# Two-layer graph attention on one core: layer 0's values in one visit, row logits ahead of the output projection, and a new order of the start

## The chip, the cores and the metric

The kernel runs on one core of a Trainium2 chip. The metric is the device time of one execution in microseconds (us); lower is better. All tensors are float32 unless said otherwise.

## The reference

There are 64 graphs of N = 256 nodes with F = 512 features and an adjacency matrix each. Two layers follow each other, each with a residual sum and a layer norm.

```python
# layer 0: graph attention with 8 heads of 64 units
feats   = einsum('bnf,hfu->bhnu', x, W)
e_self  = einsum('bhnu,hu->bhn', feats, a_self)
e_neigh = einsum('bhnu,hu->bhn', feats, a_neigh)
dense   = leaky_relu(e_self[..., :, None] + e_neigh[..., None, :], 0.2) - 1e10 * (1 - adj)
out     = relu(softmax(dense) @ feats + b)             # heads side by side: 512 wide
x       = layernorm(x + out)
# layer 1: 8 heads of 64; attention plus adjacency plus a function of it
q, k, v = x @ W_qkv                                    # 512 -> 3 x 512
attn    = 0.33 * softmax(q k^T / 8, masked) + 0.33 * adj + 0.33 * exp(-adj)
x       = layernorm(x + (attn @ v) @ W_out + b_out)
```

## The kernel before, in words

**Three graphs are in work at once.** The main loop runs b from 1 to 63. In one turn it does layer 0's attention of graph b beside layer 1's projections of graph b-1 (`attention0_beside_projections1`), then layer 1's scores of graph b-1 and the values and output of graph b-2 beside layer 0's projections of graph b+1 (`attention1_beside_projections0`). `start()` does graph 0 and the first products, `end()` the last ones. The order on every engine is written out by hand: the helper `do(stage, graph, step, ...)` issues a step and then `in_order()` ties each new instruction to the one before it on its engine. Each engine works its own list in that order, and so does SP, which issues nearly all transfers. An instruction that waits holds up everything behind it on its engine.

**The large products are made in seven parts** (`seven`, a Strassen-like scheme): p1 to p7 are products of halves and of sums of halves. They write three PSUM banks: `chain` gathers p1, p6, p7 and p4 in turn and ScalarE copies it out after each (L309); `alone` holds p2; `pair` holds p5 and then also p3. VectorE adds a bank to what ScalarE has copied (L312): `add 11` takes p2, `add 22` takes the pair after p5, `add 12` takes it after p3. So p3 must wait for `add 22`, and p6, p7 and p4 for the copy before them. This is done three times per graph: `pq` (q and k of layer 1), `pv` (its values), `pf` (features of layer 0). The adds are called qk_add, v_add and add.

**Layer 0's attention of graph b**, by the names in the profile:
- `pr` (L82): four transposes bring the two row logits of each head into rows. They read `v` (the tile V0 with features and logits), to which VectorE has added the bias (`bias`, L569). VectorE takes a maximum (L489, L490), ScalarE an exponential (L491), VectorE clamps it (L494).
- `gs`, `gb`: SP stores these 8 rows to DRAM (8 KB) and reads them back broadcast to 128 partitions (1,028 KB). `gb` has one buffer.
- `nd` (L543): the column logits less the maximum that came with `gb`; ScalarE makes `ccol` and a factor of the values from it (L550, L551), and scales the values of each head by the factor (`scaled`, L610, 16 instructions).
- `pT` (`weights`, L646): VectorE makes the unnormalised weights of a head as max(gb, ccol) times the mask, two instructions a head.
- `av` (`product`, L669): TensorE multiplies weights and values. A product writes 64 of the 128 columns of the array. Heads 0 to 3 are group 0, heads 4 to 7 group 1; each group has its own PSUM tile, and the profile shows 64 matmuls a group.
- `norm0` (L682, L684), `end` (L695): division by the sum, then relu, residual and the sums for the norm; POOL makes the mean (L346), ScalarE the squares and the norm (L351, L367). The result `x` goes to DRAM and comes back in blocks (`hs`, `hb`), and VectorE turns these to `hT` (L121) and makes the sums of halves `hC`.

**Layer 1's attention:** `pz` are the scores of a pair of heads, `p` their exponentials (ScalarE, L822), `both` the sums over two tiles (VectorE, L834), `pd` the denominators (TensorE, L842). From `zd` on (L863 to L875) VectorE inverts them; `rs` and `rb` carry them through DRAM and back, broadcast (1,024 KB). `weights` of attend1 (L901, L908) multiplies by `rb` and adds `ct`, the function of the adjacency matrix (`shared`, L456 to L471, from `adjT`). `av` at L918 are the values, `po` the output projection (L1003), summed into `x` by L931. `store` normalises graph b-3 (two L367) and sends it out.

**One turn on TensorE before:** pq p1, p2, p6, p5, p7; av group 0; pq p4, p3; av group 1; pv and pf mixed; pz 0, 1; av (L918); pz 2, 3; po; pr; po; pd.

**On VectorE before**, from pd on: zd to rec, four sums xC, nd, eight pT (heads 0 to 3), qk_add 11, qk_add 22, eight pT (heads 4 to 7), norm0 of group 0, attend1's weights 0, qk_add 12, norm0 of group 1, end, v_add 11, weights 1, v_add 22, weights 2 and so on.

**PSUM** has four banks that all small products share in turn (`ps_tile`, tag `mm`) and two tiles of two banks for `av`, `pz` and the start's broadcast `pg` (tag `sc`).

**In the start**, graph 0's and graph 1's row factors are broadcast on TensorE (`pg`, L532). Its features (L579) are done without the seven parts, and the four steps of `attention_vectors` put the products of weights and attention vectors in extra columns of the weights (`pw`, `pwa`, with `a2` from `acol`, L399). `right_factors` makes the four sums of weights for `pf` (L218 to L221, tile wf) and for `pv`.

Of the kernel before, what the change touches and what calls it, by code (L numbers as in the profile page):

```python
# [17 lines left out]
def kernel(  # L18
# [29 lines left out]
    nc = tc.nc  # L48
# [331 lines left out]
    def attention_vectors(g, step):  # L380
# [14 lines left out]
        if step == 1:  # L395
            if g == 0:
                for r in range(2):
                    rows = slice(r * U, (r + 1) * U)
                    nc.vector.tensor_copy(  # L399
                        a2[rows, :, r, :].rearrange("p g s -> p s g"), acol[rows]  # L400
                    )
# [3 lines left out]
        if step == 2:  # L405
            pwa = WA[g, "logits"]
# [22 lines left out]
    def proj0(b):  # L429
# [52 lines left out]
        def rows():  # L482
            pr = ps_tile([H, 2, N], f"pr_{b}")
            for s in range(2):
# [5 lines left out]
            nc.vector.tensor_scalar_mul(nb, grow[:, N : N + 1], -0.8)  # L490
            nc.scalar.activation(  # L491
                grow[:, :N], pr[:, 0, :], AF.Exp, bias=nb, scale=-0.8
# [115 lines left out]
        def scaled(h):  # L608
# [18 lines left out]
            rows=rows,  # L627
            columns=columns,
# [9 lines left out]
    def attend0(b):  # L638
        pT = {}

        def weights(h):

            tag = "pT" if b > 1 or h < HG else "p" if h < HG + 2 else "both"
            pT[h] = work.tile([P, T, N], FT, tag=tag, name=f"pT_{b}_{h}", bufs=4)
# [402 lines left out]
    def start():  # L1047
# [3 lines left out]
        for g in range(2):  # L1051
# [4 lines left out]
            if g == 0:  # L1056
                do("proj0", 0, "aT")
                load_adj(1)
                do("proj0", 0, "far")
# [4 lines left out]
        do("turned", 1, "xT")  # L1064
        do("proj0", 0, "columns")
        do("proj0", 0, "factors")
        attention_vectors(1, 1)
        attention_vectors(0, 2)
        attention_vectors(1, 2)
        attention_vectors(2, 0)  # L1070
        attention_vectors(3, 0)
        for h in range(2):
            do("proj0", 0, "scaled", h)
            do("attend0", 0, "weights", h)
# [4 lines left out]
        for h in range(2, HG):  # L1079
            do("proj0", 0, "scaled", h)  # L1080
            do("attend0", 0, "weights", h)
        do("proj0", 1, "features", 0, 0)
        do("proj0", 1, "features", 0, 1)
        do("attend0", 0, "product", 0, 0)
        do("attend0", 0, "product", 0, 1)
        for h in range(HG, H):
            do("proj0", 0, "scaled", h)
            do("attend0", 0, "weights", h)
        do("proj0", 1, "features", 1, 0)
        do("attend0", 0, "product", 1, 0)  # L1090
        do("attend0", 0, "product", 1, 1)
# [11 lines left out]
        for t in range(T):  # L1103
            for g in range(2):
                do("proj0", 1, "copied", t, g)
# [256 lines left out]
```

## Time and profile before

| | us |
|---|---|
| time, median of 3 runs | 2990.06 (2988.39 to 2990.53) |
| profiled execution, its own time | 2991.16 |
| its span, first to last instruction | 2989.4 |
| TensorE busy (PE) | 2957.4 |
| VectorE busy (DVE) | 2610.0 |
| ScalarE busy (ACT) | 1478.2 |
| one turn of the loop, undisturbed | 45.36 |
| first turn's pq starts at | 113.90 |
| mean granted clock of TensorE | 0.993 of full |

In the profile PE is TensorE's matmuls and PEld its weight loads, DVE is VectorE, ACT is ScalarE, SPq the queue that issues transfers. A timeline row has the start, the time from the first instruction's start to the last one's end, engine, line, operation, out<-in and the count; in brackets stands the idle time before it and what ended it. A matmul's record runs on while the next one has begun, so the length of a piece of work on TensorE is read from one row's start to the next row's start. A row of waits has the engine, the waiting line, what it waited for, the total in us, how often, and the longest. A row of windows has the stretch, its length, the busy time and count of PE, PEld, DVE, ACT and POOL, the granted clock, the DMA share and GB/s.

### The profile page before, as it was taken

How to read it: one execution, taken by the hardware profiler on the slowest of the kernel's cores; microseconds unless marked ns; L12 is line 12 of the kernel's file. 1: busy time of each engine (PE TensorE's matmuls, PEld its weight loads, DVE VectorE, ACT ScalarE, POOL GpSimd, SP SyncE). 2: the span in 40 equal slices, each digit the busy share in tenths (PEclk: the TensorE clock that was granted, in tenths of full speed). 3: DMA queues.
4: the chain of work that ended last, by engine and by line, in shares of the span. 5: the costliest groups of instructions: out<-in, count | busy, mean ns of one | idle time of the engine just before them, and what ended most of it. 6: DMA issues, size and time to landing. Idle time of an engine off the chain costs nothing.

```text
span 2989.4 us, 64730 instructions
## 1 busy us (share of the span) xinstructions
PE 2957.4 (99%) x25526; PEld 2332.6 (78%) x25526; DVE 2610.0 (87%) x5151; ACT 1478.2 (49%) x3585; POOL 183.5 (6%) x526
## 2 busy tenths in 40 slices
PE   8899999999999999999999999999999999999998
PEld 7777877877878778778778778788787787787775
DVE  5889888889888888888888888888988988888885
ACT  2454554455455455455545544554554555455443
POOL 0000000000000000000000000000000000000000
PEclk7999999999999999999999999999999999999999
DMA  6353454444444444444534544444444435445431
GB/s 120 86 128 99 109 130 98 111 126 104 111 122 103 116 109 107 125 102 110 129 96 109 133 97 111 122 104 115 110 108 123 108 105 129 97 108 133 96 93 50
DMA packets 760613, 328.22 MB, mean 110 GB/s; under 512 B 693516, under 2 KB 694268, under 8 KB 744312
## 3 DMA queue, kind: packets, MB, share of 16 engines
q1 hardware_dynamic: 758200, 323.55, 43.5%
q8 instruction: 204, 3.34, 0.5%
q14 instruction: 97, 0.79, 0.1%
q10 hardware_dynamic: 2112, 0.52, 0.1%
HBM read 256.13 MB, written 67.61 MB: 108 GB/s over the span
## 4 chain that ended last, share of the span: by engine, by line
PE 92%; DVE 3%; DMA 3%; ACT 1%; issue 1%; SPq 0%; POOL 0%; DVEq 0%; POOLq 0%
PE pq_p L300 25%; PE po L1003 14%; PE pf_p L300 13%; PE pv_p L300 12%; PE pz L813 8%; PE av L669 8%; PE av L918 7%; PE pd L842 2%; DMA gb<-gs 1%; PE pr L82 1%; DMA out_dram<-x 1%; DVE p L908 0%; DVE p L901 0%; PE pg L532 0%; DMA gs<-grow 0%
## 5 line engine op out<-in xcount | busy, mean ns | idle before, releaser
L300 PE MATMUL pq_p<-hC,wqk_sb 128*128 128x128 f32 x4096 | 487.1, 277 | 2.0 <-ACT qk L309 1.9
L300 PEld LDWEIGHTS pq_p<-hC,wqk_sb 128*128 128x128 f32 x4096 | 468.9, 192 | 7.7 <-ACT qk L309 2.9
L1003 PE MATMUL po<-wo_sb,oT 128*128 128x512 f32 x1024 | 466.3, 599 | 0.0
L646 DVE SCALAR_TENSOR_TENSOR pT<-gb,ccol,at 128x256 f32<-128x256 f32 x992 | 403.2, 480 | 17.6 <-ACT ccol L550 17.6
L300 PEld LDWEIGHTS pq_p<-hT,wqk_sb 128*128 128x128 f32 x3072 | 355.9, 193 | 29.6 <-DVE hC L278 23.9
L300 PE MATMUL pq_p<-hT,wqk_sb 128*128 128x128 f32 x3072 | 373.6, 278 | 3.2 <-DVE hT L121 1.9
L822 ACT ACTIVATE p<-pz,hide 128x512 f32<-128x512 f32 x512 | 310.8, 691 | 123.9 <-PE av L918 106.7
L1003 PEld LDWEIGHTS po<-wo_sb,oT 128*128 128x128 f32 x1024 | 184.7, 190 | 207.5 <-issue 205.8
L309 ACT COPY v<-pv_p 128x256 f32<-128x256 f32 x256 | 95.5, 373 | 472.6 <-PE pv_p L300 472.5
L351 ACT ACTIVATE junk<-x,nmean_l 128x512 bf16<-128x512 f32 x256 | 185.6, 725 | 279.9 <-POOL nmean_l L346 275.8
L908 DVE TENSOR_TENSOR p<-p,ct 128x1024 f32<-128x1024 f32 x252 | 308.7, 1225 | 8.6
L901 DVE TENSOR_TENSOR p<-p,rb 128x1024 f32<-128x1024 f32 x252 | 304.5, 1208 | 5.2 <-DMA rb<-rs 5.2
L669 PE MATMUL av<-v,pT 128*64 128x65 f32 x8192 | 267.1, 223 | 0.6 <-DVE pT L646 0.6
L669 PEld LDWEIGHTS av<-v,pT 128*64 128x64 f32 x8192 | 249.3, 138 | 16.5 <-issue 1.4
L610 ACT ACTIVATE v<-v 128x64 f32<-128x64 f32 x1024 | 260.3, 342 | 0.0
L813 PE MATMUL pz<-qk 64*128 64x256 f32 x2048 | 256.2, 389 | 0.6 <-ACT p L822 0.5
L300 PE MATMUL pf_p<-wf_sb,xC 128*128 128x264 f32 x992 | 252.3, 387 | 0.0
L300 PE MATMUL pv_p<-wv_sb,hC 128*128 128x256 f32 x1024 | 244.4, 381 | 5.5 <-DVE v L312 5.3
L813 PEld LDWEIGHTS pz<-qk 64*128 64x128 f32 x2048 | 187.1, 186 | 65.1 <-ACT p L822 25.6
L918 PE MATMUL av<-p,v 128*64 128x256 f32 x2016 | 231.7, 382 | 0.0
L300 PEld LDWEIGHTS pv_p<-wv_sb,hC 128*128 128x128 f32 x1024 | 193.4, 190 | 37.8 <-DVE v L312 10.7
L309 ACT COPY qk<-pq_p 128x512 f32<-128x512 f32 x256 | 147.7, 577 | 141.5 <-PE pq_p L300 141.4
(137 smaller groups left out, 3806.2 us busy)
## 6 DMA issues: line engine op xcount, KB each, us to landing
rb<-rs SPq DMA_DIRECT2D x63, 1024.0 KB, 4.6
gb<-gs SPq DMA_DIRECT2D x62, 1028.0 KB
xb<-in_x_dram SPq DMA_DIRECT2D x252, 128.0 KB, 4.1
x<-in_x_dram SPq DMA_DIRECT2D x63, 512.0 KB
hs<-x SPq DMA_DIRECT2D x63, 512.0 KB
hb<-hs SPq DMA_DIRECT2D x252, 128.0 KB, 3.4
out_dram<-x SPq DMA_DIRECT2D x63, 512.0 KB, 4.4
adj<-in_adj_dram SPq DMA_DIRECT2D x256, 64.0 KB, 4.5
```

The source lines that it names most:

```text
L300: matmul(d, lhsT, rhs, start=(p in FIRST and i == 0), stop=(i == len(todo) - 1), skip_group_check=True,)
L309: nc.scalar.copy(out[COPIES[p]], dst)
L351: nc.scalar.activation(junk, self.src[:, t, :], AF.Square, bias=self.nmean[:, t : t + 1], accum_out=self.rstd[:, t : t + 1],)
L610: nc.scalar.activation(V0[b][:, t, h, :U], V0[b][:, t, h, :U], AF.Copy, scale=V0[b][:, t, h, U : U + 1],)
L646: nc.vector.scalar_tensor_tensor(pT[h][:, j, :], GB[b][h], CCOL[b][:, j, h : h + 1], AT[b][:, j, :], op0=ALU.max, op1=ALU.mult,)
L669: matmul(av[r * half : (r + 1) * half, k, :], pT[h][:, j, i : i + half], V0[b][:, j, h, :UA], start=(j == 0), stop=(j == T - 1),)
L813: matmul(pz[:, r, j, :], QK[b][rows, g, 1, j * P : (j + 1) * P], QK[b][rows, g, 0, :], start=True, stop=True,)
L822: nc.scalar.activation(p[:, :, j, :], pz[:, :, j, :], AF.Exp, bias=hide[:, j, b : b + 1], scale=U**-0.5,)
L901: nc.vector.tensor_mul(p, p, REC[b][:, k : k + 2, g // 2, :] .unsqueeze(2) .to_broadcast([P, 2, T, N]),)
L908: nc.vector.tensor_add(p, p, CT[b].unsqueeze(1).to_broadcast([P, 2, T, N]))
L918: matmul(av[0][r * U : (r + 1) * U, g % 2, :], V1[b][:, j, 2 * g + r, :], PROBS[b][g][:, r, j, :], start=(j == 0), stop=(j == T - 1),)
L1003: matmul(po, oT[:, c, t * P : (t + 1) * P], wo_sb[:, c, :], start=(c == 0), stop=(c == C - 1),)
```

## The change

In the loop's first half, `av` of both groups of graph b is issued together, between p7 and p4 of `pq`. For that the weights of heads 4 to 7 are made right behind qk_add 11 and ahead of qk_add 22, and they get buffers of their own (tag `both`) in place of those of heads 0 to 3. The `store` of graph b-3 is issued ahead of p6; attend1's weights 0 come ahead of norm0, norm0 and `end` directly one behind the other, then load(b+2), then p4 and p3; attend1's weights 1 come ahead of the values.

In the second half, `rows` (pr and the maximum) is issued behind the scores 3 and ahead of `both` 2 and 3; its second part, now a step of its own called `broadcast` (exponential, clamp, gs, gb), follows them; both stand ahead of the residual sum and `po`.

In the start, all eight heads' weights of graph 0 are made directly after their row factors, and `av` of graph 0 is done there, with the columns' products (`attention_vectors`) between and behind its two groups; graph 1's features come after it. load(2), `ct` of graph 0, adjT of graph 1, `xT` of graph 2 and the sums of wf are issued earlier, ahead of `copied` of graph 1. `xT` and `xC` of graph 2 and the sums of wf no longer stand in the first turn and at the start's end (xC stays at the start's end).

```diff
             wT = WA[g] = work.tile([P, C, P], FT, tag="both", name=f"wT_{g}", bufs=4)
             nc.scalar.copy(wT, pw)
         if step == 1:
-            if g == 0:
-                for r in range(2):
-                    rows = slice(r * U, (r + 1) * U)
-                    nc.vector.tensor_copy(
-                        a2[rows, :, r, :].rearrange("p g s -> p s g"), acol[rows]
-                    )
             pwa = WA[g, "logits"] = ps_tile([P, C, 4], f"pwa_{g}")
             for c in range(C):
                 matmul(pwa[:, c, :], WA[g][:, c, :], a2[:, g], start=True, stop=True)
         if step == 2:
             pwa = WA[g, "logits"]
             for k in range(2):
                 nc.vector.tensor_copy(
...
             nb = small.tile([H, 1], FT, tag="nb", name=f"nb_{b}", bufs=2)
             nc.vector.tensor_reduce(grow[:, N : N + 1], pr[:, 1, :], AX.X, ALU.max)
             nc.vector.tensor_scalar_mul(nb, grow[:, N : N + 1], -0.8)
+            ROW.update(logits=pr, rows=grow, shift=nb)
+        def broadcast():
+            grow = ROW["rows"]
             nc.scalar.activation(
-                grow[:, :N], pr[:, 0, :], AF.Exp, bias=nb, scale=-0.8
+                grow[:, :N], ROW["logits"][:, 0, :], AF.Exp, bias=ROW["shift"], scale=-0.8
             )
             nc.vector.tensor_scalar(
                 grow[:, :N], grow[:, :N], 1.0, TINY, op0=ALU.min, op1=ALU.max
...
 
         def weights(h):
 
-            tag = "pT" if b > 1 or h < HG else "p" if h < HG + 2 else "both"
-            pT[h] = work.tile([P, T, N], FT, tag=tag, name=f"pT_{b}_{h}", bufs=4)
+            tag = "pT" if h < HG else "both" if b > 1 or h > HG + 1 else "p"
+            if (b, h) == (0, H - 1):
+                pT[h] = work.tile([P, T, N], FT, tag="rec1", name=f"pT_{b}_{h}", bufs=1)
+            else:
+                pT[h] = work.tile([P, T, N], FT, tag=tag, name=f"pT_{b}_{h}", bufs=4)
             for j in range(T):
                 nc.vector.scalar_tensor_tensor(
                     pT[h][:, j, :],
...
                 do("proj0", 0, "logits", t, g)
                 do("proj0", 0, "copied", t, g)
             if g == 0:
+                for r in range(2):
+                    rows = slice(r * U, (r + 1) * U)
+                    nc.vector.tensor_copy(
+                        a2[rows, :, r, :].rearrange("p g s -> p s g"), acol[rows]
+                    )
                 do("proj0", 0, "aT")
                 load_adj(1)
                 do("proj0", 0, "far")
...
         do("proj0", 0, "maxima")
         attention_vectors(0, 1)
         do("turned", 1, "xT")
+        load(2)
         do("proj0", 0, "columns")
         do("proj0", 0, "factors")
+        for h in range(H):
+            do("proj0", 0, "scaled", h)
+            do("attend0", 0, "weights", h)
+        for t in range(T):
+            do("attend0", 0, "product", 0, t)
         attention_vectors(1, 1)
+        attention_vectors(2, 0)
+        for t in range(T):
+            do("attend0", 0, "product", 1, t)
+        attention_vectors(3, 0)
         attention_vectors(0, 2)
         attention_vectors(1, 2)
-        attention_vectors(2, 0)
-        attention_vectors(3, 0)
-        for h in range(2):
-            do("proj0", 0, "scaled", h)
-            do("attend0", 0, "weights", h)
+        for t in range(T):
+            for g in range(2):
+                do("attend0", 0, "norm0", g, t)
+            do("attend0", 0, "end", tiles[t])
+            do("attend0", 0, "squares", tiles[t])
         attention_vectors(2, 1)
         attention_vectors(3, 1)
         attention_vectors(2, 2)
         attention_vectors(3, 2)
-        for h in range(2, HG):
-            do("proj0", 0, "scaled", h)
-            do("attend0", 0, "weights", h)
-        do("proj0", 1, "features", 0, 0)
-        do("proj0", 1, "features", 0, 1)
-        do("attend0", 0, "product", 0, 0)
-        do("attend0", 0, "product", 0, 1)
-        for h in range(HG, H):
-            do("proj0", 0, "scaled", h)
-            do("attend0", 0, "weights", h)
-        do("proj0", 1, "features", 1, 0)
-        do("attend0", 0, "product", 1, 0)
-        do("attend0", 0, "product", 1, 1)
-        do("proj0", 1, "features", 1, 1)
-        do("attend0", 0, "norm0", 0, 0)
-        do("attend0", 0, "norm0", 0, 1)
         combine_weights1(0)
-        do("attend0", 0, "norm0", 1, 0)
-        do("attend0", 0, "end", tiles[0])
-        do("attend0", 0, "squares", tiles[0])
-        do("attend0", 0, "norm0", 1, 1)
-        do("attend0", 0, "end", tiles[1])
-        do("attend0", 0, "squares", tiles[1])
+        for t in range(T):
+            for g in range(2):
+                do("proj0", 1, "features", t, g)
         do("attend0", 0, "norm", tiles[0])
+        do("proj0", 0, "shared")
+        do("proj0", 1, "aT")
+        load_rows(1)
+        do("turned", 2, "xT")
+        right_factors(wf_sb, wf12)
+        in_order()
         for t in range(T):
             for g in range(2):
                 do("proj0", 1, "copied", t, g)
-        load_rows(1)
         do("proj0", 1, "maxima")
         do("proj0", 1, "columns")
-        do("proj0", 0, "shared")
-        do("proj0", 1, "aT")
         do("proj1", 0, "from_rows", 0)
         do("attend0", 0, "norm", tiles[1])
         do("proj1", 0, "qk", "p1")
...
         do("proj0", 1, "factors")
         combine_weights1(1)
         combine_weights1(2)
-        load(2)
         load_adj(2)
         do("proj1", 0, "qk_add", 11)
         do("proj1", 0, "qk", "p6")
...
         do("proj1", 0, "qk", "p4")
         do("proj1", 0, "qk", "p3")
         do("proj1", 0, "qk_add", 12)
-        right_factors(wf_sb, wf12)
-        in_order()
+        do("turned", 2, "xC")
 
     def attention0_beside_projections1(b):
 
...
             do("proj1", b - 1, "qk", "p1")
             do("proj1", b - 1, "qk", "p2")
             do("proj0", b, "columns")
+            do("attend1", b - 3, "store")
             do("proj1", b - 1, "qk", "p6")
             for h in range(HG):
                 do("proj0", b, "scaled", h)
                 do("attend0", b, "weights", h)
-            do("attend1", b - 3, "store")
             do("proj1", b - 1, "qk_add", 11)
+            for h in range(HG, H):
+                do("proj0", b, "scaled", h)
             do("proj1", b - 1, "qk", "p5")
+            for h in range(HG, H):
+                do("attend0", b, "weights", h)
             do("proj1", b - 1, "qk", "p7")
             do("proj1", b - 1, "qk_add", 22)
-        do("attend0", b, "product", 0, 0)
-        do("attend0", b, "product", 0, 1)
-        if b > 1:
-            for h in range(HG, H):
-                do("proj0", b, "scaled", h)
-            do("proj1", b - 1, "qk", "p4")
-            for h in range(HG, H):
-                do("attend0", b, "weights", h)
-        do("attend0", b, "norm0", 0, 0)
-        do("attend0", b, "norm0", 0, 1)
-        do("attend1", b - 2, "weights", 0)
-        if b > 1:
-            do("proj1", b - 1, "qk", "p3")
-            do("proj1", b - 1, "qk_add", 12)
-        else:
-            do("turned", b + 1, "xT")
-            do("turned", b + 1, "xC")
+            do("attend1", b - 2, "weights", 0)
+        for g in range(2):
+            for t in range(T):
+                do("attend0", b, "product", g, t)
+        if b == 1:
             do("proj0", b, "shared")
             load_rowmask()
             nc.sync.dma_start(bo_bc, b_out.partition_broadcast(P))
             nc.sync.dma_start(wo_sb, w_out.rearrange("(c p) f -> p c f", p=P))
             in_order()
+        for g in range(2):
+            for t in range(T):
+                do("attend0", b, "norm0", g, t)
+        do("attend0", b, "end")
         if b + 2 < NB:
             load(b + 2)
-        do("attend0", b, "product", 1, 0)
-        do("attend0", b, "product", 1, 1)
+        if b > 1:
+            do("proj1", b - 1, "qk", "p4")
+            do("proj1", b - 1, "qk", "p3")
+            do("proj1", b - 1, "qk_add", 12)
+        do("attend1", b - 2, "weights", 1)
         do("proj1", b - 1, "values", "p1")
         do("proj1", b - 1, "values", "p2")
-        do("attend0", b, "norm0", 1, 0)
-        do("attend0", b, "norm0", 1, 1)
-        do("attend0", b, "end")
         do("proj1", b - 1, "v_add", 11)
         do("proj1", b - 1, "values", "p6")
         do("proj1", b - 1, "values", "p5")
-        do("attend1", b - 2, "weights", 1)
         do("proj1", b - 1, "values", "p7")
         do("proj1", b - 1, "v_add", 22)
         do("proj0", b + 1, "product", "p1")
...
         for g in range(HG):
             do("attend1", b - 2, "values", g)
         do("softmax1", b - 1, "scores", 2)
+        do("softmax1", b - 1, "scores", 3)
+        do("proj0", b + 1, "rows")
         do("softmax1", b - 1, "both", 2)
-        do("softmax1", b - 1, "scores", 3)
         do("softmax1", b - 1, "both", 3)
+        do("proj0", b + 1, "broadcast")
         do("attend1", b - 2, "residual")
         do("attend1", b - 2, "project", 0)
-        do("proj0", b + 1, "rows")
         do("proj1", b, "hT")
         do("attend1", b - 2, "project", 1)
         do("softmax1", b - 1, "sums")
```

More of the change, by code (lines that the diff above doesn't have):

```diff
@@ L627, in proj0 @@
             rows=rows,
+            broadcast=broadcast,
             columns=columns,
```

## The prediction

> **What bounds the kernel now.** I read the page's busy shares first, then its chain, then the waits, and last the timelines of one undisturbed graph and of the start.
>
> ```profile
> PE 2957.4 (99%) x25526; PEld 2332.6 (78%) x25526; DVE 2610.0 (87%) x5151; ACT 1478.2 (49%) x3585; POOL 183.5 (6%) x526
> PE 92%; DVE 3%; DMA 3%; ACT 1%; issue 1%; SPq 0%; POOL 0%; DVEq 0%; POOLq 0%
> ```
>
> TensorE is never free. Two things can shorten the span: fewer nanoseconds for the same matmuls, or fewer of the waits that add up to the other 32 us. The timeline of TensorE over one graph shows the first:
>
> ```profile
> 1028.14 5.52 PE L300 MATMUL pq_p<-hC,wqk_sb 128*128 128x128 f32 x48
> 1033.60 2.09 PE L669 MATMUL av<-v,pT 128*64 128x65 f32 x64
> 1035.61 2.05 PE L300 MATMUL pq_p<-hC,wqk_sb 128*128 128x128 f32 x16
> 1037.50 1.95 PE L300 MATMUL pq_p<-hT,wqk_sb 128*128 128x128 f32 x16
> 1039.38 2.09 PE L669 MATMUL av<-v,pT 128*64 128x65 f32 x64
> 1041.40 1.99 PE L300 MATMUL pv_p<-wv_sb,hT 128*128 128x256 f32 x8
> ```
>
> No row waits, and the next graph's rows stand 45.36 us later, as in most of the 60 graphs between 160 us and 2870 us. Yet these rows take longer than their matmuls. Within a row a `pq` matmul follows the last by 0.1115 us and a pair of `av` by 0.0585 us, so 80 `pq` and 64 pairs need 8.92 + 3.74 = 12.66 us; from 1028.14 to 1041.40 they take 13.26. Another 0.10 lies in the first `pv` matmul (1.83 us to the next row, where eight at 0.216 need 1.73). So two visits to the 64-column `av` cost 0.70 us beyond their work, 0.345 each: 0.09 and 0.05 on entry, 0.10 and 0.10 on exit, in the single starts.
>
> VectorE stands just behind. These rows show the weights of layer 0 (L646) and the column work ahead of them (L543):
>
> ```profile
> 1025.09 0.71 DVE L863 STREAM_TRANSPOSE zd<-pd 128x512 f32<-128x512 f32 x1
> 1028.87 0.18 DVE L543 TENSOR_TENSOR nd<-v,gb 128x16 f32<-128x16 f32 x1
> 1029.33 3.25 DVE L646 SCALAR_TENSOR_TENSOR pT<-gb,ccol,at 128x256 f32<-128x256 f32 x8 [0.28 <-ACT ccol L550]
> 1034.56 0.69 DVE L312 TENSOR_TENSOR qk<-pq_p,qk 128x512 f32<-128x512 f32 x1 [1.37 <-ACT qk L309]
> 1035.17 3.25 DVE L646 SCALAR_TENSOR_TENSOR pT<-gb,ccol,at 128x256 f32<-128x256 f32 x8
> ```
>
> The second eight weights end at 1038.4, after the place to which the second visit moves. The waits that do occur, first over the run, then with the window 165 to 2870 us:
>
> ```profile
> DVE nd L543 <- DMA gb<-gs: 10.9, 9, 2.8
> DVE x L684 <- DMA out_dram<-x: 9.9, 20, 0.8
> PEld pv_p L300 <- DVE v L312: 6.0, 13, 1.4
> ```
>
> A late broadcast `gb` delays VectorE, and the sum `v_add 22` then comes too late for the last product of the values. The periods over 45.36 add up to 4.2 us from the fourth graph on. At the start one such wait is long, and the granted clock is halved after it:
>
> ```profile
> 96.29 1.81 PE L300 MATMUL pv_p<-wv_sb,hC 128*128 128x256 f32 x4 [3.14 <-DVE v L312]
> 96.60:100.00 3.40, 3.40 (x9) 2.70 (x8) 0.42 (x1) 0.95 (x4) 1.10 (x3) 0.50 0.00 0
> ```
>
> **What the Trainium skill says.** "TensorEngine Tiling (Array Packing)", section Key Properties: changing the tiling mode, not just the tile, drains TensorE. The trace agrees on `av` (128x64 among 128x128) with the 0.345 us above; the page gives no figure. It shows no such cost around `pr` (128x8): 0.44 us for four, the po rows keep their pitch. "TensorE: Matmul & The Clock Gate", section What's actually happening: an idle window of about 3.4 us halves the clock, a busy one restores it. The trace agrees (0.50 for 3.4 us after the wait of 3.14), but also has 0.50 from 21.5 to 45.4 us with TensorE nominally busy there. "DMA: Bandwidth & Descriptors", section Anatomy of one DMA: about 2.0 us fixed before its semaphore. Here `gs` (8 KB) took 1.33 us from issue to the issue of `gb`, and I use that.
>
> **The change, part by part.**
>
> *One visit.* For graphs 2 to 63 `av` of both groups runs after p7 and before p4. One entry and one exit of two go: 62 x 0.345 = 21.4 us off the path, if nothing waits.
>
> *Does VectorE come in time?* p1, p2, p6, p5 and p7 keep their place, so the visit starts at 1033.60 as now. Without its entry and exit, a half is 1.87 us; the last head of the second group is wanted first at 1033.60 + 1.92 + 0.82 = 1036.34. VectorE: the row logits now come ahead of `both` 2 and 3, so the clamp L494 no longer waits 0.58 us for ScalarE, nor does hT stand behind that. By its durations VectorE then reaches the denominators before TensorE ends `pd` (last matmul 1024.54); `zd` starts 0.10 later (the lag of L931 behind po), at 1024.63 in place of 1025.09. From there nothing is moved: 3.78 to `nd`, 0.46 to the first weight, 3.18 for eight, 0.61 for qk_add 11, then eight more, now without the wait of 1.37: last end 1035.9, and 0.15 for the semaphore (a weight ended 83.76, its matmul started 83.91): 1036.05. Slack 0.29 us: no wait. qk_add 22 falls behind these weights, to 1036.6; p3, which waits for it, now starts at 1039.3. Its cost is nothing.
>
> *ScalarE.* Sixteen scalings in one run instead of eight and eight, behind the store's two L367 (1.52 us): 1030.9 to 1034.9 by 0.25 each; the second group is wanted at 1035.5. The copy of p7 slips from 1034.0 to 1035.0, and p4, which waits for it, to 1037.5. Nothing.
>
> *`pr` right behind the scores.* Its transposes need the bias sum L569, which ended 1014.63 + 1.25 = 1015.88; the place is 1015.96, and the lag in a recorded wait is 0.05 (108.99 to 109.05). Slack 0.02 us in every graph, held constant because ScalarE and VectorE hang there on TensorE's own matmuls. I take 0; bound: 0 to 0.1 a graph, 6 us. As the order is scores, pr, po, po, the count of switches stays.
>
> *SP and DMA.* `gs` leaves at about 1019.2 instead of 1021.85, ahead of the same `gb`, `rs`, `rb`. The latest `gb` of the run was on its way 7.7 us (1749.36 to 1757.07); with that it lands at 1028.2, before `nd` needs it. The store of b-3 and load(b+2) are issued some 3 us earlier: `x` is free in time (the 0.8 us wait at L684 goes), but they follow `rb` more closely, and `rb` is wanted at 1036.6 instead of 1039.8, some 2.5 us after its landing. `v_add 22` moves ahead of weights 2 by the earlier `end`: ready at 1046.4, where p3 of the values starts at 1048.1. So the 13 stalls should go: 3.5 of 4.2 us. POOL's mean follows `end` and is early.
>
> *The start.* Layer 0 of graph 0 now comes before graph 1's features; a2's two copies (0.34 us) move ahead of adjT, and make room later. Between 31 and 60 us TensorE gets the same matmuls in another order, VectorE does `ct` (2.4), xT of graph 2 (1.25) and wf's four sums (2.65) before `copied` instead of after. Behind the half clock this reaches graph 0's p1 between 3.8 us earlier (clock restored early) and 3.1 later; I take 0. Then wf's sums and xT, 3.9 us, are gone from VectorE's queue ahead of `v_add 22`: the wait of 3.14 goes, and the half clock behind it, 1.7: together 4.8. Late next is `gb` of graph 2: SP is still busy with hb and adj, so `nd` stays near 117.3, and the single visit waits about 2 us for its last weights, once. Net: 3 us gained, bounds +7 and -2.
>
> The end (after 2900 us) keeps its order. Sum: 21.4 + 3.5 + 3.0 = 27.9. The profiled execution took 2991.16 (span 2989.4 and 1.8 around), which gives 2963.3; it stands 1.1 above the median 2990.06, so against the median **2962 us**.
>
> **Rivals.** (A) *The switch isn't saved*: the 0.345 is not of the visit but of the rows, and comes back elsewhere. For it: no row of before shows 128 `av` in one visit within the period. Against: inside a visit the pitch is level through the change of tile. Then only stalls and start remain, 6.5 us: 2983.5. (B) *VectorE sets the visit* (the other side): the second group's weights come late each graph, because the row maximum L489 stands ahead of `both` 2 and 3 and waits for `pr`. Slack 0.29; at 0.29 + 0.345 = 0.63 us late the visit's gain is gone, at 0.73 the rest also; at 1.0 late it gives 62 x 0.365 = 22.6 lost less 6.5: 3006. For it: VectorE at 87% and a chain without reserve. Against: the walk above, and VectorE idles 3.9 us a graph now. (C) *`pr` waits for the bias* by 0.1 us: 2968. (D) *The start turns bad* by its bound and 2 us of clock more: 2969.
>
> **How the numbers follow.** Forecast 0.76 (its own range 2954 to 2974), A 0.08, B 0.06, C 0.06, D 0.04. 0.2% is 6 us, about what a measurement of this kernel can tell from no change (three runs of before span 2.1 us). All of the forecast, C, D and two thirds of A lie below 2984.1: faster 0.92; same 0.04, slower 0.04 from the rest of A and from B. The range 2951 to 2980 leaves out A's upper part and B.
>
> **What would show it.** Right: one `av` row of x128 (about 3.9 us) after 48 `pq` rows, a period of 45.02 us, `nd` without DMA waits, no `pv` stall past 160 us, `pr` right behind `pz` without a wait. Wrong: an idle before `av` x128 <-DVE pT (B), before `pr` <-DVE v (C), a period of 45.36 without waits (A), or the `pq` of graph 1 (now 113.90) starting later than 112 us (D).

## The result and the profile after

| | before | after |
|---|---|---|
| time, median (us) | 2990.3 (2988.39 to 2992.82, 4 runs) | 2965.52 (2961.33 to 2972.53, 4 runs) |
| ratio, with its 95% interval | | 0.9919 (0.9899 to 0.9939) |
| profiled execution: own time, span | 2991.16, 2989.4 | 2961.33, 2959.6 |
| undisturbed turn of the loop | 45.36 | 44.92 |
| 60 turns from the second `pd` on: what they hold above 60 undisturbed ones | 4.8 | 6.6 |
| second `pd` at | 160.30 | 154.35 |
| first `pq` of graph 1 at | 113.90 | 105.95 |

The change gained 24.8 us by the medians. The profiled execution of the changed kernel was the quickest of its four, and its span is 29.8 us shorter. Those 29.8 can be laid out by the starts of `pd`: 6.0 up to the second `pd`, 60 x 0.44 = 26.4 in the turns, less 1.8 because more is lost in disturbed turns, less 0.7 in the last two periods (40.82 + 31.05 before, 41.46 + 31.14 after).

First the timeline of TensorE over the changed part of a turn (start, length, line, operation, out<-in, count):

```profile
1047.57 2.00 PE L817 MATMUL pz<-qk 64*128 64x256 f32 x16
1049.50 0.60 PE L82 MATMUL pr<-ident,v 128*8 128x128 f32 x4
1049.94 7.03 PE L1007 MATMUL po<-wo_sb,oT 128*128 128x512 f32 x16
1056.90 1.07 PE L846 MATMUL pd<-both,ones 128*32 128x256 f32 x16
...
1061.58 5.52 PE L300 MATMUL pq_p<-hC,wqk_sb 128*128 128x128 f32 x48
1067.03 3.95 PE L673 MATMUL av<-v,pT 128*64 128x65 f32 x128
1070.91 2.05 PE L300 MATMUL pq_p<-hC,wqk_sb 128*128 128x128 f32 x16
1072.80 1.95 PE L300 MATMUL pq_p<-hT,wqk_sb 128*128 128x128 f32 x16
1074.59 1.89 PE L300 MATMUL pv_p<-wv_sb,hT 128*128 128x256 f32 x8
```

One `av` row of 128 stands where there were two of 64. From start to start it takes 3.88 us, and from the 48 `pq` to the `pv` the stretch is 13.01 where it was 13.26; the other 0.10 is in the `pv` row itself, which now takes its plain 1.73 to the next row (at 1076.32) instead of 1.83. Above it `pr` follows `pz` after 1.93 us, as `po` does where `pr` stands later (rows_between_po, below), and the sixteen `po` are one row. The weight load of `pr` does wait for the bias sum in every turn, as this row of waits in the window 165 to 2870 us shows, but while the last `pz` are still running:

```profile
PEld pr L82 <- DVE v L568: 19.9, 60, 0.3
```

VectorE in the same turn:

```profile
1058.04 0.72 DVE L867 STREAM_TRANSPOSE zd<-pd 128x512 f32<-128x512 f32 x1 [0.28 <-PE pd L846]
...
1061.83 0.18 DVE L542 TENSOR_TENSOR nd<-v,gb 128x16 f32<-128x16 f32 x1
1062.29 3.26 DVE L650 SCALAR_TENSOR_TENSOR pT<-gb,ccol,at 128x256 f32<-128x256 f32 x8 [0.28 <-ACT ccol L549]
1065.46 0.68 DVE L312 TENSOR_TENSOR qk<-pq_p,qk 128x512 f32<-128x512 f32 x1
1066.07 3.25 DVE L650 SCALAR_TENSOR_TENSOR pT<-gb,ccol,at 128x256 f32<-128x256 f32 x8
```

VectorE is free 0.28 us before `zd` can start, `nd` has no DMA wait, and the last weights end at 1069.32, 2.29 us after the visit began. The waits of TensorE's matmuls in the same window are new ones:

```profile
PE av L673 <- issue: 2.9, 5, 1.2
PE pq_p L300 <- issue: 1.9, 2, 1.6
```

"Issue" means that the engine waited for nothing that the profile shows. The waits of before (`nd` for `gb`, `x` for the store, `pv` for the sum) are gone. The longest new one inside a visit, on TensorE's timeline:

```profile
525.51 3.84 PE L673 MATMUL av<-v,pT 128*64 128x65 f32 x124
530.57 0.34 PE L673 MATMUL av<-v,pT 128*64 128x65 f32 x4 [1.22 <-issue]
530.84 2.05 PE L300 MATMUL pq_p<-hC,wqk_sb 128*128 128x128 f32 x16
```

The visit stops after 124 of its 128 matmuls, although VectorE had finished all weights at 527.8. What was late shows in the view of the DMA queues. This is the line of the whole run, and below it the same queue's line in the window 527.6 to 529.3 us (packets, MB, share of 16 engines):

```profile
q8 instruction: 204, 3.34, 0.5%
```

```profile
q8 instruction: 1, 0.02, 5.7%
```

204 packets are 16 KB each. TensorE has 51,052 matmuls and weight loads and 1,272 semaphore instructions in the trace; 3.34 MB over these is 64 bytes each, so a packet holds 256 of TensorE's instructions. That this queue is TensorE's is inferred from this count, and the places of the waits bear it out. Number TensorE's instructions from zero in the order of their starts: the first one behind a wait on "issue" of over 0.1 us always has a number that leaves 193 when divided by 256. It is so in all seven such waits of this window, and in all 69 that the ten traces of this case with any have there. So TensorE stops at one and the same place of the 256, the border between two packets.

The packet of the window began at 527.66 and took 1.56 us. The 256 instructions ahead of the stop had begun at 525.53, so it began 2.1 us behind them. From 518 us on the DMA engines carried `rb`, the store and the loads of `xb`: their busy share was 0.98 at 522 to 524 and 1.12 at 526 to 528 (it counts the whole time of a packet that begins in the stretch, so it can pass 1). TensorE went on 1.35 us after the packet was done; over the 69 waits this was 1.24 to 1.85 us. In the single starts of matmuls and loads, TensorE begins 256 instructions in no less than 6.5 us in the loop of before, and in 3.6 us where they fall into one visit of `av`.

### The profile page after: what moved, and what is told of

It is laid out like the page before. It is cut to its first block, busy times and chain, and to the rows that moved or that the text cites. A ratio compares the mean times of both kernels' runs of the same rounds, so it can differ in the third digit from the quotient of the medians.

```text
span 2959.6 us, 64542 instructions
## 1 busy us (share of the span) xinstructions
PE 2922.9 (99%) x25526; PEld 2321.6 (78%) x25526; DVE 2609.2 (88%) x5151; ACT 1468.1 (50%) x3585; POOL 185.6 (6%) x526
## 3 DMA queue, kind: packets, MB, share of 16 engines
q8 instruction: 204, 3.34, 0.5%
## 4 chain that ended last, share of the span: by engine, by line
PE 96%; DVE 1%; DMA 1%; issue 0%; ACT 0%; SPq 0%; POOL 0%; POOLq 0%; DVEq 0%
PE pq_p L300 27%; PE po L1007 15%; PE pv_p L300 13%; PE pf_p L300 13%; PE av L673 8%; PE pz L817 8%; PE av L922 8%; PE pd L846 2%; PE pr L82 1%; PE pg L531 0%; SPq L114 0%; DMA gb<-gs 0%; DMA rb<-rs 0%; DMA x<-in_x_dram 0%; DMA xb<-in_x_dram 0%
## 5 line engine op out<-in xcount | busy, mean ns | idle before, releaser
L1007 PE MATMUL po<-wo_sb,oT 128*128 128x512 f32 x1024 | 450.0, 592 | 0.0
L673 PE MATMUL av<-v,pT 128*64 128x65 f32 x8192 | 256.6, 223 | 3.7 <-issue 2.9
L609 ACT ACTIVATE v<-v 128x64 f32<-128x64 f32 x1024 | 251.6, 337 | 0.0
```

The costliest lines, as they stand in the source:

```text
L609: nc.scalar.activation(V0[b][:, t, h, :U], V0[b][:, t, h, :U], AF.Copy, scale=V0[b][:, t, h, U : U + 1],)
L673: matmul(av[r * half : (r + 1) * half, k, :], pT[h][:, j, i : i + half], V0[b][:, j, h, :UA], start=(j == 0), stop=(j == T - 1),)
L1007: matmul(po, oT[:, c, t * P : (t + 1) * P], wo_sb[:, c, :], start=(c == 0), stop=(c == C - 1),)
```

## The experiments

Each was timed beside the kernel before on the same chip, on four chips in all, so the ratios compare better than the medians. "Above" is what the 60 turns hold above 60 undisturbed ones in the profiled execution; its value for the changed kernel is 6.6, and 8.9 in a second profile.

| kernel | time, median (us) | ratio to before, 95% | turn | above |
|---|---|---|---|---|
| two_visits | 2974.14 | 0.9953 (0.994 to 0.9965) | 45.26 | 0.2 |
| rows_between_po | 2994.77 | 1.0015 (1.0007 to 1.0024) | 45.24 | 20.7 |
| old_start | 2970.56 | 0.9942 (0.993 to 0.9955) | 44.92 | 11.5 |
| store_behind_p7 | 2960.22 | 0.9902 (0.9888 to 0.9915) | 44.92 | 4.7 |
| load_behind_visit | 2962.77 | 0.9907 (0.9894 to 0.9921) | 44.92 | 2.2 |
| store_twice | 2957.26 | 0.989 (0.9876 to 0.9903) | 44.92 | 3.3 |
| rows_between_po_xC_late | 2991.71 | 1.0009 (1.0001 to 1.0016) | 45.02 to 45.16 | |
| after_again | 2964.69 | 0.9919 (0.9906 to 0.9932) | 44.92 | 8.9 |
| visit_only | 3000.80 | 1.0034 (1.0023 to 1.0045) | 45.24 | 20.8 |
| rows_ahead_only | 2979.23 | 0.9967 (0.9954 to 0.998) | 45.26 | 4.2 |
| load_behind_visit_from_2 | 2958.51 | 0.9892 (0.9879 to 0.9905) | 44.92 | 2.5 |
| rows_between_po_load_late | 2985.15 | 0.9985 (0.9978 to 0.9992) | 45.24 | 9.3 |

### The visit alone undone

```diff
         for g in range(2):
             for t in range(T):
                 do("attend0", b, "product", g, t)
+            if b > 1 and g == 0:
+                do("proj1", b - 1, "qk", "p4")
...
         if b > 1:
-            do("proj1", b - 1, "qk", "p4")
             do("proj1", b - 1, "qk", "p3")
```

> The changed kernel with one thing undone: av of group 1 follows p4 of pq instead of av of group 0, so that TensorE visits the 64-column av twice a graph; all other engines keep their order. If the gain is the switch (0.345 us a visit), the undisturbed period goes from 44.92 to 45.26 and some 21 us are lost in 62 graphs. The eight new TensorE stalls of the changed kernel (6.6 us in its profiled run) are, by my theory, waits for its own instructions, which one visit uses up faster than two; with the visit broken by 32 slower instructions some should go, 3 to 5 us. Together 2965.5 + 21 - 4 = about 2982. Rival A (the switch is not of the visit, or it comes back elsewhere): period 44.92 to 45.0, time 2962 to 2967.

TensorE's timeline:

```profile
1016.53 5.52 PE L300 MATMUL pq_p<-hC,wqk_sb 128*128 128x128 f32 x48
1021.98 2.09 PE L673 MATMUL av<-v,pT 128*64 128x65 f32 x64
1024.00 2.05 PE L300 MATMUL pq_p<-hC,wqk_sb 128*128 128x128 f32 x16
1025.98 2.09 PE L673 MATMUL av<-v,pT 128*64 128x65 f32 x64
1027.99 2.05 PE L300 MATMUL pq_p<-hT,wqk_sb 128*128 128x128 f32 x16
1029.88 1.89 PE L300 MATMUL pv_p<-wv_sb,hT 128*128 128x256 f32 x8
```

`pv` stands 13.35 us after the start of the 48 `pq`, where it was 13.01 with one visit. The turn is 45.26, to the hundredth what the switch asks for, and rival A is out. The Trainium skill's "TensorEngine Tiling (Array Packing)", section Key Properties, has a change of the tiling mode drain TensorE; these runs put 0.34 us on a visit. But only 8.6 us are lost in the median (10 by the ratios), not 17: every disturbed turn of the loop is gone (0.2 us above the undisturbed turns), so that the single visit costs back a good part of what it brings. Here 256 instructions take at least 5.3 us. In the profiles, 20.4 are lost in 60 turns, 6.4 won back there, 2.5 up to the second `pd` (151.85; the start is the same in both, so this is the spread of single executions) and 0.9 in the last two periods, which makes the 10.6 between the spans.

### Rows put back between the two `po`

```diff
-        do("proj0", b + 1, "rows")
         do("softmax1", b - 1, "both", 2)
         do("softmax1", b - 1, "both", 3)
-        do("proj0", b + 1, "broadcast")
         do("attend1", b - 2, "residual")
         do("attend1", b - 2, "project", 0)
+        do("proj0", b + 1, "rows")
+        do("proj0", b + 1, "broadcast")
```

> The changed kernel with rows and broadcast (pr, maximum, exponential, clamp, gs, gb) put back between the two po. Two theories on its price. My reading of the traces: po straight behind pz has a slow second matmul (533 instead of 429 ns), which pr between them avoids, so 0.10 us a turn or 6 us come back; VectorE gets to zd 0.46 us later, which takes the slack of 0.29 us before the last weights of the one visit, so av waits 0.17 us a graph, 10 us more, and gb is late in some graphs (1 to 5 us). Together 2982 to 2987, period about 45.2. Rival: VectorE has more room than I worked out and only the 0.10 counts: period 45.02, 2971 to 2973. If pr's place costs nothing at all, as the prediction had it, 2965 and 44.92.

```profile
1008.75 2.00 PE L817 MATMUL pz<-qk 64*128 64x256 f32 x16
1010.68 3.70 PE L1007 MATMUL po<-wo_sb,oT 128*128 128x512 f32 x8
1014.21 0.60 PE L82 MATMUL pr<-ident,v 128*8 128x128 f32 x4
1014.65 3.60 PE L1007 MATMUL po<-wo_sb,oT 128*128 128x512 f32 x8
1018.18 1.07 PE L846 MATMUL pd<-both,ones 128*32 128x256 f32 x16
...
1028.31 4.18 PE L673 MATMUL av<-v,pT 128*64 128x65 f32 x128
1032.42 2.05 PE L300 MATMUL pq_p<-hC,wqk_sb 128*128 128x128 f32 x16
```

From `pz` to `pd` it is 9.43 us against 9.33 in the changed kernel: the eight `po` behind `pz` take 3.53 us to the next row, where eight at 0.43 need 3.44. In the single starts the second `po` follows the first by 0.533 us and the others by 0.43, and with `pr` between `pz` and `po` no start is long. The visit takes 4.11 us instead of 3.88, since VectorE comes 0.23 later than needed (I had 0.17). These two make 0.33, and the turn is 0.32 longer. The disturbed turns I had put far too low: they hold 20.7 us. So this place alone costs 29 us, and one visit without the earlier rows is slower than the kernel before.

> As rows_between_po (rows and broadcast between the two po), and the four sums xC, which stand ahead of nd and the weights on VectorE, moved behind qk_add 22: VectorE reaches the weights 1.5 us earlier. If the 0.22 us that av takes longer in rows_between_po is VectorE's lateness, the period falls from 45.24 to 45.02 (44.92 and the 0.10 of the slow second matmul of po), some 13 us; late instruction packets may stay, so 2972 to 2982. If av waits there for something else, 45.24 and about 2994.

```diff
             do("proj1", b - 1, "qk_add", 22)
+            if b + 1 < NB:
+                do("turned", b + 1, "xC")
             do("attend1", b - 2, "weights", 0)
...
-        if b + 2 < NB:
-            do("turned", b + 2, "xC")
```

(This is on top of rows_between_po.) The quickest turns are 45.02, as they should be if VectorE was late; most are 45.05 to 45.16. The time hardly follows, 2991.71. With VectorE 1.5 us earlier, the next to be late is `gb`; the waits of the two kernels on this line are 8.0 us in 8 graphs in rows_between_po and here

```profile
DVE nd L542 <- DMA gb<-gs: 77.9, 59, 2.9
```

and TensorE's disturbances stay. Moving the row logits did two things at once: it gave VectorE its reserve, and it put `gb` in time.

### Each part by itself

> The loop's first half of the changed kernel (one visit of av) without the two other parts: rows and broadcast between the two po and the start as in the kernel before. If the parts depend on each other as rows_between_po suggests (the visit has no reserve on VectorE, 0.23 us late a graph, and gb, rb, the store and the loads then meet at the refill of TensorE's instructions, some 15 to 25 us of stalls), it is slower than the kernel before: 2995 to 3003. Rival, each part worth its own price: 62 x (0.345 - 0.23) = 7 us faster than before, 2981 to 2985.

This kernel has the changed order of the loop's first half, and `rows`, `broadcast` and the start as before. It is 10.9 us slower than the kernel before: turns of 45.24 gain 7.2 us over 60 turns, disturbed turns cost 16.0 more (20.8 against 4.8), and the second `pd` stands 1.9 later.

> The kernel before with rows (pr) put behind pz 3 and ahead of both 2 and 3, and broadcast ahead of the residual sum; two visits and the old start stay. By the slow second matmul of po behind pz (0.10 us a turn) 6 us go, and with gb on its way 2.6 us earlier most of the 4 us of its stalls: 2979 to 2982, period 45.26. If pr's place costs nothing by itself, as the prediction had it, only the stalls go: 2985 to 2988, period 45.36.

```diff
-        do("softmax1", b - 1, "both", 2)
         do("softmax1", b - 1, "scores", 3)
+        do("proj0", b + 1, "rows")
+        do("softmax1", b - 1, "both", 2)
         do("softmax1", b - 1, "both", 3)
+        do("proj0", b + 1, "broadcast")
         do("attend1", b - 2, "residual")
         do("attend1", b - 2, "project", 0)
-        do("proj0", b + 1, "rows")
```

(On the kernel before.) The turn is 45.26: the 0.10 is of `pr`'s place and needs nothing else of the change. The time falls by 10.7 us, more than the 6 of the turn and, in this profile, not because fewer turns are disturbed (4.2 us against 4.8); where the other 4 are is not settled, the profiled execution of this kernel being itself 6.2 above its median. Its trace has no wait of `nd` for `gb` left, and still 13 waits of `pv` for a late sum, as many as before. Each stands in a turn in which `norm0` waited for the store:

```profile
DVE x L689 <- DMA out_dram<-x: 12.9, 21, 1.1
```

> The changed kernel's loop with the start of the kernel before (and its xT, xC of graph 2 in the first turn). By the marks in the two traces the new start gains 7.3 us at the first pd and gives 1.8 back in the first period, so this kernel should be about 6 us slower than the changed one: 2971. By the prediction's sum (3 us) it would be 2968.5; if the start gained nothing, 2965.5. Period 44.92 as in the changed kernel.

The new start is worth 5.0 us by the medians. In the profiles the second `pd` is at 158.19 here, at 154.35 and 155.80 in the changed kernel's two, so 2.4 to 3.8 us lie there; the rest is more disturbed turns in this one. (The 1.8 of the expectation, given back in the first period, are 1.3 by the starts of `pd`: 50.72 before, 52.05 after.) Against before, this kernel is visit and earlier rows without the new start: -19.5 us. Each of the two alone gave +10.9 and -10.7, together +0.2. In the undisturbed turn they gave 0.12 and 0.10 alone and 0.44 together, which is 13 us of the difference over 60 turns; the rest is mostly disturbed turns. The visit pays only behind the earlier rows.

### What the disturbed turns wait for

> The changed kernel with store of graph b-3 issued behind qk_add 22 instead of ahead of p6, so that SP's 512 KB store and the four loads behind it leave some 7 us later, after the visit. In the changed kernel a packet of the instruction queue (16 KB, 256 of TensorE's instructions) comes up to 6 us after its predecessor is begun where these transfers are under way, and the eight stalls (6.6 us) follow such packets. If that is their cause they go: 2957 to 2960, no av or pq stall past 160 us, less spread between runs. Rival (the stalls have another cause than the transfers): they stay, 2963 to 2967. The undisturbed period stays 44.92.

```diff
             do("proj0", b, "columns")
-            do("attend1", b - 3, "store")
...
             do("proj1", b - 1, "qk_add", 22)
+            do("attend1", b - 3, "store")
```

5.3 us faster than the changed kernel, with two issue waits of `av` left (0.8 us). The 6 us of the expectation are not in the trace of the changed kernel: between 165 and 2870 us a packet begins at most 2.6 us, and is done at most 3.9 us, after the 256 instructions ahead of it begin. A new wait took some of the gain: `norm0` writes the buffer from which the store still reads, and `v_add 22` comes too late for `pv` in six turns.

```profile
DVE x L688 <- DMA out_dram<-x: 66.9, 60, 2.8
```

> The changed kernel with its store left where it is, and load(b+2) held back: VectorE writes one column of the new xb behind attend1's weights 0 (a memset of 128 x 1, about 0.06 us), so that SP issues the four 128 KB loads after the visit, some 8 us later. If TensorE's stalls are late instruction packets behind these transfers, most of the 6.6 us of stalls past 160 us go, and norm0 does not wait for the store as it did with the store late: 2957 to 2960, below the 2960 of store_behind_p7. If only the store's 512 KB count, stalls stay and it is 2964 to 2967. The period stays 44.92.

> As load_behind_visit (the four loads of xb held until attend1's weights 0 are done), but the first turn left as in the changed kernel. load_behind_visit lost 3.6 us in its first period (55.21 against 51.6), which should come back, and the stalls past 160 us stay near 2 us: 2957 to 2960. If the first period had other causes: 2961 to 2964.

```diff
+        if 1 < b < NB - 2:
+            XB[b + 2] = io.tile([P, C, N // B, B], FT, tag="xb", name=f"xb_{b + 2}", bufs=1)
+            nc.vector.memset(XB[b + 2][:, 0, 0, 0:1], 0.0)
+            load_blocks(XB[b + 2], x[b + 2])
+            in_order()
         for g in range(2):
             for t in range(T):
                 do("attend0", b, "product", g, t)
...
-        if b + 2 < NB:
+        if b == 1:
             load(b + 2)
```

The first of the two held the load in turn 1 as well and lost 3.6 us there (a first period of 55.21 us); the second left that turn alone. SP's timeline of the second:

```profile
518.98 0.32 SPq L888 DMA_DIRECT2D rb<-rs  x1
520.54 0.39 SPq L1024 DMA_DIRECT2D out_dram<-x  x1
529.08 2.84 SPq L114 DMA_DIRECT2D xb<-in_x_dram  x4
```

and of the changed kernel in its turn with the wait:

```profile
520.72 0.32 SPq L888 DMA_DIRECT2D rb<-rs  x1
522.28 0.39 SPq L1024 DMA_DIRECT2D out_dram<-x  x1
522.72 4.89 SPq L114 DMA_DIRECT2D xb<-in_x_dram  x4
```

With the loads 10.1 us behind `rb` instead of 2.0, the disturbed turns hold 2.2 and 2.5 us above in place of 6.6 and 8.9, and TensorE's issue waits over 0.1 us sum to 0.9 us in the second. The seven places at which the changed kernel waited show how. The packet begins 1.0 to 1.6 us after the 256 instructions ahead of it in six of them (in the changed kernel 1.4 to 2.4) and 2.7 in the last (2.6), and the gaps from start to start at these places sum to 1.7 us instead of 6.4. At 2958.51 (2956.53 to 2960.37, against 2961.33 to 2972.53) this version beats both kernels, by 31 us and by 7, and its runs lie closer together.

> The changed kernel with the output of graph b-3 stored twice to the same place (512 KB more traffic ahead of the visit; no engine but SP has more to do). If late instruction packets behind bulk transfers cause the stalls, packets come 1.5 to 2 us later, the stalls grow and more turns have one: 15 to 35 us slower than the changed kernel, 2980 to 3000. If the transfers have no part in it, 2964 to 2968. The undisturbed period stays 44.92 in both.

```diff
-            nc.sync.dma_start(out[b].rearrange("(t p) f -> p t f", p=P), X1[b])
+            for _ in range(2):
+                nc.sync.dma_start(out[b].rearrange("(t p) f -> p t f", p=P), X1[b])
```

This went the other way: 8.3 us faster than the changed kernel, 7.4 than its second measurement on the same chip (after_again). SP shows why; below its rows stands its row of waits over the whole run:

```profile
517.86 0.31 SPq L888 DMA_DIRECT2D rb<-rs  x1
519.42 5.36 SPq L1025 DMA_DIRECT2D out_dram<-x  x2
524.83 3.24 SPq L114 DMA_DIRECT2D xb<-in_x_dram  x4
```

```profile
SPq L1025 <- DMA out_dram<-x: 298.3, 63, 6.6
```

The second store writes where the first does, so SP waited until the first was done, and the loads behind it left 6.97 us after `rb` instead of 2.00. It doubled the store but spread the traffic, so as a dose of traffic it was no test, and my expectation had the mechanism of the queue wrong. Read as it ran, it agrees with load_behind_visit: loads later, 3.3 us above.

> rows_between_po (rows and broadcast between the two po, one visit) with the four loads of xb held until attend1's weights 0 are done, from the second turn on. In rows_between_po the 60 periods hold 20.7 us above 60 times the undisturbed 45.24. If those are late instruction packets behind the store and the loads, as in the changed kernel, 12 to 16 us of them go: 2979 to 2984, period 45.24. If gb and rb, which the later rows bring closer to the visit, hold the packets up by themselves: 2989 to 2995.

```diff
+        if 1 < b < NB - 2:
+            XB[b + 2] = io.tile([P, C, N // B, B], FT, tag="xb", name=f"xb_{b + 2}", bufs=1)
+            nc.vector.memset(XB[b + 2][:, 0, 0, 0:1], 0.0)
+            load_blocks(XB[b + 2], x[b + 2])
+            in_order()
...
-        if b + 2 < NB:
+        if b == 1:
             load(b + 2)
```

(On rows_between_po.) Of its 20.7 us 11.4 go, 9.6 by the medians, a little less than expected. TensorE has no issue wait over 0.1 us left; the waits that remain are those of `pq` for ScalarE's copy (4.4 us) and of `nd` for `gb` (6.0). So about half of what its disturbed turns lose (11.4 of 20.7) is the loads' doing as well; what the other half comes from was not tested.

> The changed kernel itself once more, beside the three others on the same chip, for the size of its stalls and the spread of its runs: 2961 to 2973, with 5 to 12 us of stalls past 160 us in the profiled run, six graphs (270 us) or a multiple apart, since a graph takes some 830 instructions of TensorE and a packet holds 256.

2964.69 (2963.66 to 2970.72), with 8.9 us above. Its waits stand at 260.8, 531.2 and 801.8, then 1342.4, and another row of them at 1297.6, 1568.9, 1839.1, 2108.9 and 2648.7: steps of 270 us or twice that, each about six turns. In the loop a turn has 396 matmuls, as many loads and 20 semaphore instructions, 812 in all (fewer than the 830 of the expectation); six turns are 19 packets and 8 instructions, so the cut between packets comes back to nearly the same place of the turn. Which of these turns wait, and how long, differs from run to run, and so does the time. That it follows what the DMA engines carry just then is argued from the kernels with later loads, not shown turn by turn.

## Why the prediction was right, and where it was not

**The visit** (21.4 us): right. Undoing it alone gave 0.34 a turn, and the walk of VectorE was right to 0.01 us: last weights 2.29 us after the visit's start, worked out as 2.3, and no wait of `av` for VectorE. Rival B had the place, but the reason the wrong way round: it feared that the earlier rows make the second group's weights late, and it is without them that the visit is 0.23 us late in each turn.

**`pr` right behind the scores** (0): a term that was mis-sized, with 0.10 a turn or 6 us. The step was "the count of switches stays". The count did stay, but the second of the `po` behind `pz` came 0.533 us after the first in the profile of before already, and I read only that `po` kept its pitch around `pr`. The tie with the bias cost nothing, though it is as close as worked out: only the weight load of `pr` waits for it, and `pr` starts 1.93 us after `pz`. So rival C is out.

**SP and DMA** (3.5 of 4.2 us to go): this step failed in its sum. The waits that it names are gone: `nd` no longer waits for `gb`, the wait for the store (now L688) is gone, and no `pv` waits for a sum in the window. But it asked of the store and the loads that leave earlier only whether their buffers are free and whether `rb` is in time. They now fall into the visit, and the visit uses up TensorE's instructions faster than before; 6.6 to 8.9 us of waits for instructions took the place of 4.8. Instead of 3.5 gained, 1.8 were lost in the profiled run. One of its readings was also too simple: it laid the late `v_add 22` to a late `gb`. In the profile of before nine of the 13 turns with such a wait have one for the store and none for `gb`, and rows_ahead_only has the 13 without any wait for `gb`. The two errors, +6 and -5, nearly cancel. That the median came out only 3.5 us from the forecast is luck in this respect, though either error alone would have stayed in the forecast's own range.

**The start** (3, from -2 to +7): the medians give 5.0. The profiles give 4.7 and 5.2 if the stretch ahead of graph 0's first `pq` is left out: from there to the second `pd` it is 102.51 us in old_start, and 97.83 and 97.27 in the two profiles of the changed kernel. (It is 100.84 before, so the new order of the turns costs some 1.7 us here.) By terms: the wait of 3.14 and the half clock behind it went as worked out; from the first `pv` to the first `pz` it took 17.57 us before and 12.47 now, 5.1 against the 4.8 of the sum. The single wait for the late `gb` of graph 2 came, at another place than the visit: `nd` waits for it, ScalarE's copy of p6 stands behind `ccol`, which needs `nd`, and so TensorE stands 2.31 us ahead of p7's matmuls.

```profile
90.76 1.03 PE L300 MATMUL pv_p<-wv_sb,hC 128*128 128x256 f32 x4
...
109.62 3.74 PE L300 MATMUL pq_p<-hC,wqk_sb 128*128 128x128 f32 x32
115.67 3.46 PE L300 MATMUL pq_p<-hC,wqk_sb 128*128 128x128 f32 x16 [2.31 <-ACT qk L309]
```

```profile
114.61 0.19 DVE L542 TENSOR_TENSOR nd<-v,gb 128x16 f32<-128x16 f32 x1 [3.34 <-DMA gb<-gs]
```

The `pq` of graph 1 starts at 105.95, and at 108.24 in the second profile, so rival D is out.

What the change does before 60 us, taken as 0, cannot be read from one profile: graph 0's first `pq` was at 59.46 and 55.68 in two kernels with the old start (before and old_start), and at 56.52 and 58.53 in the two profiles of the changed kernel. The granted clock between 30 and 40 us differed between them: 0.50, 0.68, 0.79 and 0.55 in this order.

**The end** (0): 0.7 lost.

## What to carry to other kernels

Gathering dense small matmuls saves a switch each, but it also makes TensorE use up its instructions faster; look in the DMA view whether its instruction packets have to get past bulk transfers just then, and move those transfers behind the dense stretch. A reorder that takes an engine's slack may be worth nothing by itself: measure it together with the step that makes the slack. Here the visit alone cost 10.9 us, the earlier rows alone gained 10.7, and the two together gained 19.5. And read the single starts at every change of matmul shape, not at the one that the change is about: 0.10 us behind `pz` was a quarter of the gain in a turn.

## What was not expected of the hardware

- TensorE can stop for its own instructions with every operand ready. They come 256 at a time (16 KB) in one DMA packet of 0.9 to 1.6 us. Where it waited, the packet had begun 1.3 to 3.4 us after the 256 instructions ahead of it, and TensorE went on no sooner than 1.24 us after its end. In one visit of `av` 256 instructions last only 3.6 us, and in the changed kernel waits of up to 1.6 us follow.
- The second `po` (128x128) behind `pz` (64x128) starts 0.533 us after the first instead of 0.43. With four `pr` (128x8) between them this is gone, and nothing shows in its place.
